# Pairwise bilinear products: the depth instead of the batch on the partitions, and input tiles loaded in four pieces behind stores

## The chip, the cores and the metric

The kernel runs on one core of a Trainium2 chip. The metric is the device time of one execution in microseconds (us): the median of three runs of the kernel before is 1301.92 us (1301.0 to 1302.68). A core has a matrix engine (PE, with its weight loads shown apart as PEld), a vector engine (DVE), a scalar engine (ACT), GpSimd (POOL) and a sync engine (SP) that here only issues transfers. Transfers between the device memory (HBM) and the on-chip memory (SBUF, 128 partitions) are carried by 16 DMA engines that all queues share. The matrix engine writes to a small accumulator memory (PSUM).

## What is computed

```python
def _L0_rec_ref(x, W):                    # x: (4096, 32, 64), W: (64, 64), float32
    vid = jnp.einsum('bfd,de->bfe', x, W)
    idx_i, idx_j = jnp.triu_indices(32, k=1)
    return x[:, idx_i, :] * vid[:, idx_j, :]
```

For each of 4096 batch rows, the 32 fields of depth 64 are projected by one 64 x 64 matrix, and each field i is multiplied, element by element, with the projection of each later field j. There are 496 such pairs. The input is 33.55 MB, the output 4096 x 496 x 64 floats, which is 520.09 MB. All is float32.

## The kernel before

**Tiles.** The batch lies on the partitions. A group g is 256 batch rows, two (r = 0, 1) on each partition, so that a partition holds 16 KB of input (R x F x D floats); there are 16 groups. The unit of work is a tile t = 2g + r: 128 batch rows, one on each partition, with 32 x 64 inputs and 496 x 64 outputs per partition. There are 32 tiles.

**Loads** (`load`, L62 to L73). The first three groups are loaded at the start on the sync queue, the first of them in three parts (L67, L68, L70). The other 13 are issued from ACT (L72), each after the second tile of the group three before, as one transfer of 2 MB with 16 KB per partition. Three buffers hold the groups.

**Projection** (`project`, L80 to L107). In a tile with the batch on the partitions the depth must first be brought onto the partitions. For each four pairs of fields, PE transposes four 128 x 128 blocks (L88), ACT copies them from PSUM to `xT` (L91), PE multiplies each field with W in float32 (two matmuls of 64 columns for a pair, on the upper and the lower 64 rows, L96), and ACT copies the result to `vid` (L103). `vid` has two buffers, so a tile's projection can run while DVE works on the tile before.

**Products** (`products`, L109 to L117). DVE does one multiplication for each field i: field i, repeated, times the projections of all later fields. That is 31 instructions to a tile.

**Stores.** The 496 pairs of a tile are cut by fields into three slots, `(0, 6)`, `(6, 13)` and `(13, 31)`: 171, 154 and 171 pairs. Each slot has its own output buffer from a pool of three, and is stored by one DMA on the sync queue (L137) once DVE has filled it. The first two tiles are stored in smaller parts (`FIRST`, `SECOND`).

**Order.** Within each engine the instructions run in program order. A store waits on SP for DVE's slot; DVE waits for the store that last used the slot's buffer. Loads from group 3 on wait in ACT's program among the copies, and travel in a queue of their own beside the stores' queue.

Of the kernel before, what the change touches and what calls it, by code (L numbers as in the profile page):

```python
# [1 line left out]

# [5 lines left out]

F32 = mybir.dt.float32
ALU = mybir.AluOpType  # L10

SLOTS = [(0, 6), (6, 13), (13, 31)]

FIRST = [(13, 31, [24, 18, 13]), (6, 13, [10, 8, 6]), (0, 6, [4, 2, 0])]
SECOND = [(0, 6, [2, 4, 6]), (6, 13, [8, 10, 13]), (13, 31, [18, 31])]


@with_exitstack  # L20
def pairwise_bilinear_kernel(
    ctx: ExitStack,
    tc: tile.TileContext,
    x: bass.AP,
    w: bass.AP,
    out: bass.AP,
):
    nc = tc.nc
    P = 128
    B, F, D = x.shape  # L30
    NP = F * (F - 1) // 2

    R = 2
    G = B // (P * R)


    TPB = 4
    GRP = F // 2 // TPB
    SLOT = 171
    AHEAD = 3  # L40

    xg = x.rearrange("(g p r) f d -> g p r f d", p=P, r=R)
    og = out.rearrange("(g p r) n d -> g p r n d", p=P, r=R)
    off = [i * (F - 1) - i * (i - 1) // 2 for i in range(F)]

    const = ctx.enter_context(tc.tile_pool(name="const", bufs=1))
    xpool = ctx.enter_context(tc.tile_pool(name="x", bufs=AHEAD))
    tpool = ctx.enter_context(tc.tile_pool(name="xT", bufs=1))
    vpool = ctx.enter_context(tc.tile_pool(name="vid", bufs=2))
    opool = ctx.enter_context(tc.tile_pool(name="out", bufs=3))  # L50
    ps_t = ctx.enter_context(
        tc.tile_pool(name="ps_t", bufs=4, space=bass.MemoryType.PSUM)
    )
    ps_v = ctx.enter_context(
        tc.tile_pool(name="ps_v", bufs=2, space=bass.MemoryType.PSUM)
    )

    w2 = const.tile([P, D], F32)
    nc.scalar.dma_start(out=w2[0:D, :], in_=w)
    nc.scalar.dma_start(out=w2[D : 2 * D, :], in_=w)  # L60

    def load(g):  # L62
        queue = nc.sync if g < AHEAD else nc.scalar
        xt = xpool.tile([P, R, F, D], F32, tag="x", name=f"x_{g}")
        if g == 0:
            h = F // 2
            nc.sync.dma_start(out=xt[:, 0, h:, :], in_=xg[g][:, 0, h:, :])  # L67
            nc.sync.dma_start(out=xt[:, 0, :h, :], in_=xg[g][:, 0, :h, :])  # L68
            for r in range(1, R):
                nc.sync.dma_start(out=xt[:, r], in_=xg[g][:, r])  # L70
        else:
            queue.dma_start(out=xt, in_=xg[g])  # L72
        return xt  # L73

    loaded = [load(g) for g in range(AHEAD)]

    ident = const.tile([P, P], F32)
    make_identity(nc, ident)

    def project(xt, r, tag, order):  # L80

        xT = tpool.tile([P, F // 2, P], F32, tag="xT", name=f"xT_{tag}")
        vid = vpool.tile([P, F // 2, 2, D], F32, tag="vid", name=f"vid_{tag}")
        for g in order:
            pairs = range(g * TPB, (g + 1) * TPB)
            pt = ps_t.tile([P, TPB, P], F32, tag="pt", name=f"pt_{tag}_{g}")
            for k, pair in enumerate(pairs):
                nc.tensor.transpose(  # L88
                    pt[:, k, :], xt[:, r, 2 * pair : 2 * pair + 2, :], ident
                )  # L90
            nc.scalar.copy(xT[:, g * TPB : (g + 1) * TPB, :], pt)  # L91

            pv = ps_v.tile([P, 2, 2 * TPB, D], F32, tag="pv", name=f"pv_{tag}_{g}")
            for k, pair in enumerate(pairs):
                for h in range(2):
                    nc.tensor.matmul(  # L96
                        pv[:, h, k, :],
                        lhsT=xT[h * D : (h + 1) * D, pair, :],
                        rhs=w2[h * D : (h + 1) * D, :],
                        start=True,  # L100
                        stop=True,
                    )
            nc.scalar.copy(  # L103
                vid[:, g * TPB : (g + 1) * TPB].rearrange("p k h e -> p h k e"),
                pv[:, :, :TPB, :],
            )
        return vid.rearrange("p g h e -> p (g h) e")  # L107

    def products(xt, vid, ot, base, r, fields):  # L109
        for i in fields:  # L110
            n = F - 1 - i
            nc.vector.tensor_tensor(  # L112
                ot[:, off[i] - base : off[i] - base + n, :],
                xt[:, r, i : i + 1, :].to_broadcast([P, n, D]),
                vid[:, i + 1 :, :],
                ALU.mult,
            )  # L117

    for g in range(G):
        xt = loaded[g]  # L120
        for r in range(R):
            t = g * R + r
            first = t == 0
            vid = project(xt, r, t, range(GRP - 1, -1, -1) if first else range(GRP))
            plan = FIRST if first else SECOND if t == 1 else None
            for s, (lo, hi) in enumerate(SLOTS):
                if plan:
                    lo, hi, ends = plan[s]
                else:
                    ends = [hi]  # L130
                ot = opool.tile([P, SLOT, D], F32, tag="o", name=f"o_{t}_{s}")
                base = off[lo]
                at = hi if first else lo
                for e in ends:
                    a, b = (e, at) if first else (at, e)
                    products(xt, vid, ot, base, r, range(b - 1, a - 1, -1) if first else range(a, b))
                    nc.sync.dma_start(  # L137
                        out=og[g][:, r, off[a] : off[b], :],
                        in_=ot[:, off[a] - base : off[b] - base, :],
                    )  # L140
                    at = e
        if g + AHEAD < G:
            loaded.append(load(g + AHEAD))


_INS = ["r_x", "L0_rec_W"]
_OUTS = [((4096, 496, 64), "float32")]


# [21 lines left out]
```

## Time and profile before

| what | value |
|---|---|
| median of three runs | 1301.92 us |
| the profiled execution's own time | 1302.08 us |
| its span, first to last instruction | 1300.3 us |
| DVE busy | 1132.8 us, 992 instructions |
| PE busy / PEld busy | 336.3 us / 315.8 us |
| ACT busy | 136.4 us |
| packets of the sync queue, of the ACT queue | 526.39 MB, 27.30 MB |

The page gives busy time by engine, then the span in 40 slices (busy tenths of each engine, the clock granted to PE, and what the DMA engines moved), then queues, the chain of work that ended last, the groups of instructions and the DMA issues. An engine's idle time is listed with what released it. A DMA's time runs from its issue to its landing, so it includes the time in which it stands in its queue.

### The profile page before, as it was taken

To read this page: it belongs to the slowest core of one execution; us is meant where nothing else is said; L and a number is where in the kernel's file an instruction comes from. 1 tells how busy PE (TensorE), PEld (TensorE's weight loads), DVE (VectorE), ACT (ScalarE), POOL (GpSimd) and SP (SyncE) were. 2 spreads that over 40 slices of the span, in tenths; PEclk is the share of its full clock that TensorE was granted. 3 is DMA by queue.
4 is the path that set the end of the run, shared out by engine and by line. 5 is a ranking of instruction groups with operands and counts; after the bars stand their busy time and mean duration, and the time that the engine had idled before them with its cause. 6 is when DMAs were issued, how large, how long until landed. Compare 5 with 4: busy or idle time off the path is not lost.

```text
span 1300.3 us, 6845 instructions
## 1 busy us (share of the span) xinstructions
PE 336.3 (26%) x2560; PEld 315.8 (24%) x2560; DVE 1132.8 (87%) x992; ACT 136.4 (10%) x257; POOL 0.7 (0%) x6
## 2 busy tenths in 40 slices
PE   7333213332033320333203332033330233321000
PEld 6333203332033320333203332033330223311000
DVE  6999979889798897988979899798987979999991
ACT  3111101111011110111101111001110011110000
POOL 0000000000000000000000000000000000000000
PEclk9555555555555555555555555555555555555555
DMA  9999999999999999999999999999999999999997
GB/s 384 430 421 439 428 430 436 423 432 430 428 429 430 434 422 436 435 422 433 433 429 431 423 434 424 430 435 428 433 426 427 437 421 430 434 433 431 436 431 318
DMA packets 18193, 554.12 MB, mean 426 GB/s; under 512 B 2160, under 2 KB 2160, under 8 KB 2544
## 3 DMA queue, kind: packets, MB, share of 16 engines
q1 hardware_dynamic: 16128, 526.39, 94.5%
q10 hardware_dynamic: 2032, 27.30, 4.9%
q8 instruction: 20, 0.33, 0.1%
q14 instruction: 13, 0.11, 0.0%
HBM read 33.59 MB, written 520.09 MB: 426 GB/s over the span
## 4 chain that ended last, share of the span: by engine, by line
DMA 62%; DVE 35%; issue 1%; PE 0%; DVEq 0%; ACT 0%
DMA out_dram<-o 61%; DVE o L112 35%; DMA x<-in_r_x_dram 0%; PE pt L88 0%; PE pv L96 0%; DVEq L166 0%; DVEq L112 0%; ACT vid L103 0%
## 5 line engine op out<-in xcount | busy, mean ns | idle before, releaser
L112 DVE TENSOR_TENSOR o<-x,vid 128x64 f32<-128x64 f32 (+30 forms) x992 | 1132.8, 1219 | 141.3 <-DMA out_dram<-o 130.2
L96 PE MATMUL pv<-w,xT 64*128 64x64 f32 x2048 | 230.0, 413 | 862.0 <-ACT vid L103 827.8
L96 PEld LDWEIGHTS pv<-w,xT 64*128 64x128 f32 x2048 | 218.2, 320 | 878.6 <-ACT vid L103 837.7
L103 ACT COPY vid<-pv 128x512 f32<-128x512 f32 x128 | 72.1, 587 | 1060.2 <-DVE o L112 971.3
L88 PE MATMUL pt<-ident,x 128*128 128x128 f32 x512 | 108.8, 397 | 5.4 <-DMA x<-in_r_x_dram 5.4
L88 PEld LDWEIGHTS pt<-ident,x 128*128 128x128 f32 x512 | 97.6, 212 | 9.0 <-issue 5.3
L91 ACT COPY xT<-pt 128x512 f32<-128x512 f32 x128 | 66.4, 610 | 5.7 <-PE pt L88 5.6
L91 ACT ACT_TABLE_LOAD x1 | 1.3, 1283 | 2.0 <-issue 2.0
masks.py:199 POOL TENSOR_SCALAR_AFFINE_SELECT ident<-ident 128x128 f32<-128x128 f32 x1 | 0.3, 292 | 0.1
masks.py:197 POOL MEMSET ident<- 128x128 f32 x1 | 0.2, 204 | 0.3 <-POOLq L157 0.3
L157 POOL MEMSET const-bfloat16-1.0<- 128x1 bf16 x1 | 0.1, 102 | 0.0
L157 POOL MEMSET const-uint8-127<- 128x1 uint8 x1 | 0.1, 102 | 0.0
L157 POOL MEMSET const-float32-0.0<- 128x1 f32 x1 | 0.1, 99 | 0.2 <-issue 0.2
L157 POOL MEMSET const-float32-1.0<- 128x1 f32 x1 | 0.1, 99 | 0.0
## 6 DMA issues: line engine op xcount, KB each, us to landing
out_dram<-o SPq DMA_DIRECT2D x60, 5472.0 KB, 25.5
out_dram<-o SPq DMA_DIRECT2D x30, 4928.0 KB, 28.4
x<-in_r_x_dram ACTq DMA_DIRECT2D x13, 2048.0 KB, 23.0
out_dram<-o SPq DMA_DIRECT2D x2, 2560.0 KB, 12.8
x<-in_r_x_dram SPq DMA_DIRECT2D x2, 2048.0 KB, 14.4
out_dram<-o SPq DMA_DIRECT2D x2, 1952.0 KB, 11.6
out_dram<-o SPq DMA_DIRECT2D x2, 1920.0 KB, 11.6
out_dram<-o SPq DMA_DIRECT2D x2, 1824.0 KB, 11.6
```

The costliest lines, as they stand in the source:

```text
L88: nc.tensor.transpose(pt[:, k, :], xt[:, r, 2 * pair : 2 * pair + 2, :], ident)
L91: nc.scalar.copy(xT[:, g * TPB : (g + 1) * TPB, :], pt)
L96: nc.tensor.matmul(pv[:, h, k, :], lhsT=xT[h * D : (h + 1) * D, pair, :], rhs=w2[h * D : (h + 1) * D, :], start=True, stop=True,)
L103: nc.scalar.copy(vid[:, g * TPB : (g + 1) * TPB].rearrange("p k h e -> p h k e"), pv[:, :, :TPB, :],)
L112: nc.vector.tensor_tensor(ot[:, off[i] - base : off[i] - base + n, :], xt[:, r, i : i + 1, :].to_broadcast([P, n, D]), vid[:, i + 1 :, :], ...
L157: nc = _bacc.Bacc("TRN2", target_bir_lowering=False, num_devices=1)
```

## The change

**Layout.** The depth now lies on the partitions. The input array is handed to the device as 16 tiles of 128 x 32 x 128: partition p below 64 holds depth p of one batch block of 128 rows, partition 64 + p depth p of another block 2048 rows on. The output is laid out likewise, 128 x 496 x 128 per tile, and brought back to the reference's order after the run. The rearrangement of both arrays is not part of the device's program. A tile is therefore twice as large: 32 x 128 inputs (16 KB) and 496 x 128 outputs per partition, and there are 16 tiles.

**Projection.** No transposes, no identity, no `xT`. W stands twice, on partitions 0 to 63 and 64 to 127. For each group of 8 fields PE does four matmuls of 512 columns (two field quads by two halves of the partitions), each 64 x 64 weights, and ACT copies the 1,024 results per partition to `vid` at once. Four groups make a tile.

**Products and stores.** The 496 pairs are cut into six slots of 83 pairs (the last of 81) whatever the field borders, with one store each, and still three output buffers. A slot holds 83 x 128 floats per partition, 42.5 KB. DVE has 36 instructions to a tile. The first tile is done backwards and stored in 14 smaller parts.

**Loads.** Everything goes through the sync queue, whose order is now that of the program text (`manual_schedule`). Tile 0 is loaded in four pieces of 8 fields, tile 1 in two. From tile 2 on, a tile comes in four pieces of 8 fields (4 KB per partition, 512 KB in all), piece n issued directly behind the store of slot n of the tile before, n = 1 to 4, slots being counted from 0. There are two input buffers instead of three.

The core of the diff:

```diff
-    R = 2
-    G = B // (P * R)
-    TPB = 4
-    GRP = F // 2 // TPB
-    SLOT = 171
-    AHEAD = 3
+    GRP = 8
+    NGRP = F // GRP
+    BANK = 512 // C
+    SLOT = 83
+    AHEAD = 2
+    PIECES = 4
...
+    ctx.enter_context(tc.manual_schedule(engines={mybir.EngineType.SP}))
...
+    def load(t, lo, hi):
+        if t not in xs:
+            xs[t] = xpool.tile([P, F, C], F32, tag="x", name=f"x_{t}")
+        nc.sync.dma_start(out=xs[t][:, lo:hi, :], in_=x[t][:, lo:hi, :])
...
-                nc.tensor.transpose(
-                    pt[:, k, :], xt[:, r, 2 * pair : 2 * pair + 2, :], ident
-                )
-            nc.scalar.copy(xT[:, g * TPB : (g + 1) * TPB, :], pt)
...
+            pv = psum.tile([P, GRP, C], F32, tag="pv", name=f"pv_{t}_{g}")
+            for b in range(0, GRP, BANK):
+                f = g * GRP + b
                 for h in range(2):
+                    half = slice(h * D, (h + 1) * D)
                     nc.tensor.matmul(
-                        pv[:, h, k, :],
-                        lhsT=xT[h * D : (h + 1) * D, pair, :],
-                        rhs=w2[h * D : (h + 1) * D, :],
+                        pv[half, b : b + BANK, :],
+                        lhsT=w2[half, :],
+                        rhs=xs[t][half, f : f + BANK, :],
                         start=True,
                         stop=True,
                     )
+            nc.scalar.copy(vid[:, g * GRP : (g + 1) * GRP, :], pv)
...
+        fields = [i for i in range(F - 1) if off[i] < b and off[i + 1] > a]
+        for i in reversed(fields) if backwards else fields:
+            s, e = max(a, off[i]), min(b, off[i + 1])
+            j = i + 1 + s - off[i]
             nc.vector.tensor_tensor(
+                ot[:, s - base : e - base, :],
+                xs[t][:, i : i + 1, :].to_broadcast([P, e - s, C]),
+                vid[:, j : j + e - s, :],
                 ALU.mult,
             )
...
+    for g in reversed(range(NGRP)):
+        load(0, g * GRP, (g + 1) * GRP)
+    load(1, F // 2, F)
+    load(1, 0, F // 2)
...
+            for n, base in enumerate(bases):
+                top = min(base + SLOT, NP)
+                ot = opool.tile([P, SLOT, C], F32, tag="o", name=f"o_{t}_{n}")
+                products(t, vid, ot, base, base, top)
+                store(t, ot, base, base, top)
+                if 1 <= n <= PIECES and t + 1 < NT and t + 1 not in (0, 1):
+                    load(t + 1, (n - 1) * F // PIECES, n * F // PIECES)
...
+    x = x.reshape(2, NT, C, F, D).transpose(1, 0, 4, 3, 2).reshape(NT, 2 * D, F, C)
```

## The prediction

> **What bounds the kernel now.** I read the page first: the busy shares, the DMA row of the 40 slices, the bytes, the chain.
>
> ```profile
> span 1300.3 us, 6845 instructions
> ...
> PE 336.3 (26%) x2560; PEld 315.8 (24%) x2560; DVE 1132.8 (87%) x992; ACT 136.4 (10%) x257; POOL 0.7 (0%) x6
> ...
> DMA  9999999999999999999999999999999999999997
> ...
> HBM read 33.59 MB, written 520.09 MB: 426 GB/s over the span
> ...
> DMA 62%; DVE 35%; issue 1%; PE 0%; DVEq 0%; ACT 0%
> ```
>
> The DMA engines are full in every slice but the last. DVE's 35% of the chain is no limit: the chain alternates between a store and the slot that it set free. The next view says so, the waits.
>
> ```profile
> DVE o L112 <- DMA out_dram<-o: 130.2, 71, 4.7
> ```
>
> DVE waits 130.2 us in all for stores to free buffers, so it has that much in hand. Bytes and bandwidth set the time, and the change moves the same bytes. Next, busy times by stretch, for stretches between the starts of a third slot; after the span the columns are PE, PEld, DVE, ACT and POOL busy (instructions), clock, DMA share, GB/s.
>
> ```profile
> 1111.63:1149.05 37.42, 10.74 (x80) 10.20 (x80) 35.38 (x31) 4.20 (x8) 0.00 (x0) 0.55 1.01 435
> 1149.05:1186.48 37.43, 7.36 (x64) 6.98 (x64) 35.38 (x32) 4.20 (x8) 0.00 (x0) 0.50 1.00 432
> 1030.32:1111.63 81.31, 21.23 (x160) 19.98 (x160) 70.94 (x62) 8.40 (x16) 0.00 (x0) 0.54 1.00 429
> ```
>
> The first two are single tiles after the last load: 16.25 MB of stores in 37.43 us, or 434.2 GB/s. The third is two tiles and one 2 MB load: 81.31 - 2 x 37.43 = 6.45 us for a load that at 434.2 GB/s would be 4.83. Over the chain from 182.33 to 1111.63 (23 tiles, 11.5 loads) a load costs (929.3 - 860.9) / 11.5 = 5.95 us.
>
> Then the DMA issues, for how deep the queue is (count, size, median us to landing):
>
> ```profile
> out_dram<-o SPq DMA_DIRECT2D x60, 5472.0 KB, 25.5
> x<-in_r_x_dram ACTq DMA_DIRECT2D x13, 2048.0 KB, 23.0
> ```
>
> A store of 12.9 us lands 25.5 us after its issue: when it is issued, one other store is still ahead. Loads run three groups ahead, and no DVE wait for a load or for `vid` is listed but one at the start. Last, the timeline of one projection (start, length), for prices:
>
> ```profile
> 1086.08 1.07 ACT L103 COPY vid<-pv 128x512 f32<-128x512 f32 x2 [35.68 <-DVE o L112]
> 1086.72 3.68 PE L96 MATMUL pv<-w,xT 64*128 64x64 f32 x32 [31.15 <-ACT vid L103]
> 1111.63 12.73 DVE L112 TENSOR_TENSOR o<-x,vid 128x1152 f32<-128x1152 f32 x18 [1.85 <-DMA out_dram<-o]
> 1124.92 22.65 DVE L112 TENSOR_TENSOR o<-x,vid 128x1984 f32<-128x1984 f32 x13 [0.56 <-DMA out_dram<-o]
> ```
>
> From the two DVE rows (10,944 elements in 18 instructions, 20,800 in 13) I solve 1.043 ns per element and 73 ns per instruction.
>
> **What the skill says.** The Trainium skill, "DMA: Bandwidth & Descriptors", section "Queues, rings and completion order": on each DMA engine a queue's descriptors are taken in ring order, and an engine goes round robin between queues. The trace agrees on the second: a load of 4.8 us of work takes 23.0 us to land beside the stores. The first is what I rest on for loads put into the stores' own ring; no run of before shows it. The same page, "Where 436 GB/s comes from": the fabric's ceiling is 435.2 GB/s. The 434.2 above agrees, so nothing is left to win on stores. "FP8 and Floating Point Precision", "TensorE Precision Notes": a true float32 matmul takes four passes; "TensorE: Matmul & The Clock Gate", Part 3: matmuls on different row groups overlap. 32 matmuls of 64 columns in 3.68 us at half clock are 115 ns each; four passes at the page's cold 1.2 GHz would be 213 ns alone, so pairs did overlap.
>
> **The change part by part.**
>
> *Removed: 512 transposes, 128 `xT` copies.* They stand beside DVE and DMA work (ACT idles 971 us for DVE), gain 0. In the open they would cost a tile its 16 transposes (3.4 us a burst) and four copies; they are not in the open.
>
> *DVE.* 16 x 496 x 128 elements at 1.043 ns are 1059.9 us; 581 instructions (41 in tile 0, 36 in each other) at 73 ns are 42.4: 1102 us instead of 1133. Per tile 68.9 us against 80 us of DMA: DVE isn't the bound, gain 0.
>
> *Stores.* Same bytes. A slot of 10,624 elements is 5.44 MB, 12.53 us at 434.2 GB/s; the last, 10,368, is 12.23. 0 net.
>
> *Loads, as work.* 14 tiles in 56 pieces of 512 KB, 1.21 us each. Before shows 5.95 us for 2 MB, mixed with stores; I take that, and an allowance of 0.2 for the shorter rows: 14 x 0.2 = +3. Lower end: in one ring the mixing excess of 1.1 goes, -15. Upper end: each piece, not each load, pays 1.1, so +3.3 a tile, +46.
>
> *SP.* Its 56 load issues cost some 0.35 us each, in a queue that waits for DVE most of the time; hidden by the stores queued ahead. But a piece is now behind its store's wait: it can't be issued before DVE finished slot n, and can't be served before store n is through.
>
> *The new wait, which decides.* Slot 0 of tile t+1 begins with field 0, whose 31 products need all of `vid`, so also fields 24 to 31: piece 4, which stands behind store 4 of tile t. When piece 4 lands, the ring holds store 5 alone, which was ready long before (DVE is held three buffers back). DVE stands still until the projection is done, then has a whole slot to compute before SP, queued behind it, can issue the next store. From the end of piece 4 in the ring:
> - receipt of the landing 0.4: the last store's last packet starts at 1297.0 to 1297.5 and takes 12.9 / 8 = 1.6, so ends at 1298.6 to 1299.1; it lands at 1274.2 + 25.3 = 1299.5.
> - PE wakes 0.1 later (first load landed at 0.74 + 4.5 = 5.2, PE started at 5.36).
> - Four matmuls of 512 columns: 2,048 columns, as many as the 3.68 us burst above. I take 3.7. Lower end 1.8, at full clock (or if the old burst was held by its weight loads); upper end 7.2, if the two halves don't overlap.
> - ACT's copy of 1,024: one of 512 takes 0.585 (0.535 back to back), so 0.585 + 512 x 0.833 ns at the ScalarE page's rate of one element per cycle ("ScalarE: Activation LUTs", section "What ACT_TABLE_LOAD costs") = 1.0; with hand-overs 1.2.
> - DVE slot 0: 10,624 x 1.043 ns + 3 x 73 ns = 11.3.
> - Issue to first packet 1.0 (first load issued at 0.74; first packet in the window 1.5 to 2.0).
>
> Sum 17.7 us. Store 5 covers 12.2. The DMA engines stand idle 5.5 us at each entry into tiles 2 to 15 (tile 1 is loaded at the start): 14 x 5.5 = +77. It does not come back later: after the gap the ring only refills, and at the end of the next tile the same piece stands there again. Within a tile there is no second gap: slot 1 takes 11.4 us and store 0 12.5.
>
> *Start and end.* DVE can begin at about 9.5 us instead of 11.15 (piece landed 5.2, W at 1.32 + 5.6 = 6.9, PE at full clock 1.8, copy 1.0), but the ring has 4.2 MB to load (9.7 us) instead of 6.3 before it needs stores, and small first stores follow each other about 1 us apart: I put +3. The end is as now (5.31 instead of 5.47 MB last).
>
> Sum on the profile's span: 1300.3 + 3 + 77 + 3 = 1383.3. The profiled execution took 1302.08, 1.8 more than its span, and 0.2 more than the median of the runs; so 1385.
>
> **Rivals.**
> - *Faster: pieces overtake.* If the reads of a piece proceed while the store ahead in the same ring is still being written, piece 4 lands up to 12.5 us earlier, with stores 4 and 5 to cover the chain: 24.8 against 17.7, no gap. The mixing excess may go too: 1302 + 3 + 3 - 15 = 1293. It decides from 5.5 us of overtaking on. For it: read and write are different directions. Against: ring order, and loads at the start landed one after another (4.5, 5.5, 7.5 us from issue).
> - *PE twice as slow.* The halves now write the same PSUM banks on different partitions; if they run one after the other, 7.2 instead of 3.7: +49, 1434.
> - *Pieces dear.* Each switch between store and load costs the 1.1: 1385 + 43 = 1428.
> - *It doesn't do what it says.* The instruction order of the changed program shows the pieces behind stores 1 to 4 and the waits as described, so no chance is put on this.
>
> **Numbers.** Forecast, the gap of 3.5 to 7 us a tile, 0.75 (its own range 1352 to 1410: PE at 1.8 gives -27, a cheaper load -15, not both likely in full; the upper side by symmetry of the load price); PE serial 0.13; dear pieces 0.07; overtaking 0.05. A measurement of this kernel tells about 0.2%, 2.6 us. Faster 0.04, within 0.2% 0.01, slower 0.95. Leaving out overtaking and the corners where two dear cases meet, the range is 1352 to 1434.
>
> **What would show it.** In the profile after: GB/s that dips once in about 86 us instead of a flat row; DVE idle for `vid` some 14 times, each ending with ACT's copy, which waited for PE, which waited for the load; 17 to 18 us from the end of piece 4 to the first packet of the next store; mean GB/s near 401. If DVE waits mainly for stores and the DMA row is full, the step with the wait is wrong. If the gap is there but other than 5.5, PE's burst is the first term to look at. If stretches with no gap move less than 429 GB/s, the price of pieces is.

## The result, and the profile after

The changed kernel takes 1416.14 us (median of four runs, 1414.2 to 1416.86), against 1301.97 us for the kernel before: a ratio of 1.0875, 95% interval 1.0856 to 1.0894. It is slower, by 114 us where 83 were forecast, and inside the stated range. The profiled execution took 1414.2 us, its span is 1412.3 us, 112.0 us longer than before's.

The page of the kernel after: span, busy times, the DMA row of the 40 slices with what was moved, the bytes, and the chain that ended last.

```profile
span 1412.3 us, 2185 instructions
...
PE 222.2 (16%) x512; PEld 56.7 (4%) x512; DVE 1099.4 (78%) x581; ACT 66.1 (5%) x65; POOL 0.2 (0%) x4
...
DMA  8999989799898998979979899798998979989799
GB/s 338 431 426 416 410 352 423 340 420 423 333 428 357 420 426 345 429 342 420 422 327 431 348 414 428 328 432 351 408 428 337 426 342 414 430 348 409 341 443 401
...
HBM read 33.59 MB, written 520.09 MB: 392 GB/s over the span
...
DVE 57%; DMA 27%; issue 9%; PE 4%; ACT 1%; SPq 0%; DVEq 0%
```

The bytes are the same. The row that was full is now full except for a dip to between 327 and 357 GB/s once in two or three slices, that is once a tile. In the chain the DMA share has fallen from 62% to 27%, and what is left of it is loads, not stores. The list of waits names the new one:

```profile
PE pv L72 <- DMA x<-in_r_x_dram: 1094.8, 56, 99.6
DVE o L88 <- ACT vid L79: 292.8, 15, 21.2
```

Before, DVE waited 130.2 us for stores and for `vid` only at the start. Now it never has to wait for a store; it waits for `vid` 15 times, the start and 14 entries into a tile, some 20 us each. The chain at one of them (start and length in us):

```profile
669.69 27.09 DMA x<-in_r_x_dram
...
696.91 3.69 PE pv L72 x8
...
700.63 1.02 ACT vid L79
...
701.67 0.04 DVE o L88
```

Piece 4 lands at 696.8, PE does its burst of matmuls, ACT its copy, and DVE starts slot 0 at 701.67. SP can issue the next store only when that slot is done, at 713.07. The stretches around it (columns as in the prediction: span, busy times of PE, PEld, DVE, ACT, POOL, then clock, DMA share, GB/s; a packet counts where it starts):

```profile
709.00:713.50 4.50, 0.00 (x0) 0.00 (x0) 4.50 (x3) 0.00 (x0) 0.00 (x0) 0.50 0.00 0
713.50:714.00 0.50, 0.00 (x0) 0.00 (x0) 0.50 (x2) 0.00 (x0) 0.00 (x0) 0.50 2.59 1105
```

For 4.5 us no DMA engine starts a packet, while DVE computes; then all start at once. The packet records of the whole run hold 14 stretches after the start in which no engine has a packet in flight, 5.0 to 5.2 us each.

From the landings in the trace I take the step from one transfer's last landing to the next one's. A tile's ten steps, mean over 13 tiles (s = store, l = load piece), and the same for three of the kernels below:

```
             s0     s1     l1    s2     l2    s3     l3    s4     l4    s5     tile
after        17.98  13.63  2.01  12.75  1.42  12.79  1.55  12.69  1.63  12.26  88.72
late         17.95  13.62  2.37+1.25+1.26  12.97  12.53  12.63  1.27  12.26    88.09
shift        13.44 (l 1.26)  13.46 (1.24)  13.49 (1.25)  13.47 (1.25)  12.55  12.24  83.66
bunch        12.55  12.55  1.23+1.56+1.25+1.35  12.68  12.54  12.54  12.24     80.50
```

In the last tile of the kernel after, which has no loads, stores 1 to 4 take 12.6 each. So store 0, with 17.98, carries a gap of 5.4 us. The rest of a tile is 83.3; six stores alone are 75.3; the 2 MB load costs 8.0 us in its four places, 6.6 in its own steps and 1.4 in the stores next to them. The account of the 112 us is then: gaps 14 x 5.4 = 75; loads 14 x (8.0 - 5.95) = 29; stores, 75.3 against 2 x 37.43 a tile, 16 x 0.44 = 7; together 111.

### The profile page after: what moved, and what is told of

It is laid out like the page before. It is cut to its first block, busy times and chain, and to the rows that moved or that the text cites. A ratio compares the mean times of both kernels' runs of the same rounds, so it can differ in the third digit from the quotient of the medians.

```text
span 1412.3 us, 2185 instructions
## 1 busy us (share of the span) xinstructions
PE 222.2 (16%) x512; PEld 56.7 (4%) x512; DVE 1099.4 (78%) x581; ACT 66.1 (5%) x65; POOL 0.2 (0%) x4
## 4 chain that ended last, share of the span: by engine, by line
DVE 57%; DMA 27%; issue 9%; PE 4%; ACT 1%; SPq 0%; DVEq 0%
DVE o L88 57%; DMA x<-in_r_x_dram 26%; PE pv L72 4%; ACT vid L79 1%; SPq L96 0%; DMA w<-in_L_rec_W_dram 0%; DVEq L154 0%
## 5 line engine op out<-in xcount | busy, mean ns | idle before, releaser
L88 DVE TENSOR_TENSOR o<-x,vid 128x1408 f32<-128x1408 f32 (+15 forms) x581 | 1099.4, 1973 | 292.8 <-ACT vid L79 292.8
L72 PE MATMUL pv<-x,w 64*64 64x512 f32 x512 | 222.2, 1013 | 1100.2 <-DMA x<-in_r_x_dram 1094.8
L79 ACT COPY vid<-pv 128x1024 f32<-128x1024 f32 x64 | 64.8, 1012 | 1255.4 <-PE pv L72 1255.4
L72 PEld LDWEIGHTS pv<-x,w 64*64 64x64 f32 x512 | 56.7, 206 | 1264.3 <-issue 1253.5
```

What stands on the lines that cost most here:

```text
L72: nc.tensor.matmul(pv[half, b : b + BANK, :], lhsT=w2[half, :], rhs=xs[t][half, f : f + BANK, :], start=True, stop=True,)
L79: nc.scalar.copy(vid[:, g * GRP : (g + 1) * GRP, :], pv)
L88: nc.vector.tensor_tensor(ot[:, s - base : e - base, :], xs[t][:, i : i + 1, :].to_broadcast([P, e - s, C]), vid[:, j : j + e - s, :], ALU ...
```

## Experiments

All keep the changed kernel's layout. Beside each median stands its ratio to the kernel before, taken in the same set of runs. In each of these kernels 14 tiles, 2 to 15, are loaded behind stores (13 where there is a third input buffer); in two expectations I took 15.

**shift: the pieces one store earlier.**

```diff
-                if 1 <= n <= PIECES and t + 1 < NT and t + 1 not in (0, 1):
-                    load(t + 1, (n - 1) * F // PIECES, n * F // PIECES)
+                if n < PIECES and t + 1 < NT:
+                    load(t + 1, n * F // PIECES, (n + 1) * F // PIECES)
```

> The same four pieces, one store earlier: behind stores 0 to 3, tile 2 starting it from tile 1. Gap theory (the DMA engines idle 5.4 us at each of 14 tile entries because only store 5 covers the chain piece 4 - projection - slot 0): stores 4 and 5 now cover 24.9 us against a chain of about 17.7, the gap goes, 1416 - 14 x 5.4 = 1340 us (1332 to 1350). Rival, the time is lost in the switches between stores and pieces and not in a gap: as many switches, so 1405 to 1416.

Measured 1343.63 us, ratio 1.0323 (1.0307 to 1.0338). As the gap theory said: 72.5 us of the 114 go with one place in the queue. DVE still waits for `vid` at every tile, but less than in the changed kernel, and waits for stores again:

```profile
DVE o L88 <- ACT vid L79: 135.5, 15, 11.6
DVE o L88 <- DMA out_dram<-o: 77.4, 27, 3.2
```

Of the first, nine us a tile are left. No stretch in which all engines are without a packet is left after the start, but a smaller gap is. From about 335 us on each tile has 1.1 to 2.4 us in which only two to four of the 16 engines have a packet in flight; one of them (at full use the DMA share, the last figure but one, is about 1):

```profile
753.30:754.90 1.60, 0.00 (x0) 0.00 (x0) 1.60 (x2) 0.00 (x0) 0.00 (x0) 0.50 0.12 52
```

A transfer gives 16 landing signals, which I take as one from each engine, and it has landed with the last of them. From about 335 us on the fifteenth signal comes 2 to 6 us after the fourteenth, and the last one 5 to 10 us after it. So piece 4 is late on two engines, DVE starts late, and the other 14 run out of work for a moment although stores 4 and 5 stand behind the piece. Averaged over the 16 engines this is 23 us of idle time between 180 and 1280 us, against 0.2 in the next kernel.

**bunch: all four pieces behind store 1.**

```diff
+                if n == 1 and t + 1 < NT:
+                    for m in range(PIECES):
+                        load(t + 1, m * F // PIECES, (m + 1) * F // PIECES)
```

> The four 512 KB pieces one after the other behind store 1, so one switch between stores and loads per tile instead of four, rows still of 4 KB. Gap theory: stores 2 to 5 cover the chain, no gap, at most 1340. If the excess of the pieces (8.0 us a tile, with what the stores before them lose, against 4.8 at the rate of the stores) is a price per switch: 1.5 us a tile once, about 1316. If it is a price of rows of 4 KB or of each DMA: as the four spread pieces, 1340.

Measured 1301.47 us, ratio 1.0000 (0.9991 to 1.0009). Lower than any of the expectations: as fast as the kernel before. The same four DMAs with the same 4 KB rows cost 42 us less than in shift. So neither the rows of 4 KB nor the number of DMAs is what makes the pieces dear in shift. Two things differ: there they stand apart, and the last of them stands two stores later. The run pairs, below, bears on both. DVE's list is that of a kernel bound by stores again:

```profile
DVE o L88 <- DMA out_dram<-o: 156.0, 85, 7.4
DVE o L88 <- ACT vid L79: 11.3, 1, 11.3
```

**one: the tile in one DMA with 16 KB per partition behind store 1.**

```diff
+                if n == 1 and t + 1 < NT:
+                    load(t + 1, 0, F)
```

> The whole tile of 2 MB in one DMA with 16 KB per partition behind store 1. If the price is per switch: as the bunch, about 1316. If it is per row or per DMA: the bunch at 1340 and this one near 1310 to 1316.

Measured 1311.25 us, ratio 1.0073 (1.0058 to 1.0088). Against expectation this form is dearer than the bunch, by 9.8 us over 14 tiles. That counts against my allowance for shorter rows in the prediction: it had the wrong sign. The edit changes two things, the length of the rows and the number of DMAs, and no run separates them. Much of the difference lies on few engines: by the signals of the last store 11 of 16 end by 1296.9 us and the last at 1308.3, in the bunch 13 by 1295.4 and the last at 1298.5.

**half: slot 0 stored in two halves.**

```diff
+                mid = base + 41 if n == 0 else top
+                products(t, vid, ot, base, base, mid)
+                store(t, ot, base, base, mid)
+                if n == 0:
+                    products(t, vid, ot, base, mid, top)
+                    store(t, ot, base, mid, top)
```

> Pieces stay behind stores 1 to 4; only slot 0 of each tile is stored in two halves (41 and 42 pairs), so that SP can issue after 5.7 us of DVE work instead of 11.3. Gap theory: the chain shrinks from 17.7 to 12.1, store 5 covers 12.2, the gap goes (0 to 0.5 us a tile), about 1340 to 1346. If the chain before the slot (landing, projection) is what counts, or something else holds the ring, nothing changes: 1412 to 1418.

Measured 1379.34 us, ratio 1.0597 (1.0581 to 1.0613): 37 us gained, half of what I expected, so neither reading holds as written. The landings say why. The first half comes without a gap (6.21 us, as much as it takes to carry), but store 1 now takes 16.4 us, and a gap stands there, in the trace at 708.3 for 2.6 us with no packet in flight on any engine:

```profile
709.00:710.50 1.50, 0.00 (x0) 0.00 (x0) 1.50 (x2) 0.00 (x0) 0.00 (x0) 0.50 0.00 0
711.00:724.00 13.00, 0.00 (x0) 0.00 (x0) 13.00 (x6) 0.00 (x0) 0.00 (x0) 0.50 0.93 377
```

DVE started at 688.68 and needs 22.7 us for slots 0 and 1, however they are stored; the issue takes 1.0 more, and 5.3 had passed since the end of piece 4: 29.0 us, for which store 5 and both halves give 12.2 + 12.6 us of cover. That leaves 4.2 us; measured are 3.9 (16.4 less a store of 12.55). What I had overlooked is the second slot: a late DVE must win back its lead slot by slot, at 12.5 - 11.4 us each. A finer first store moves the gap and shortens it, it doesn't remove it.

**twice: the last group's matmuls done twice.**

```diff
-                for h in range(2):
+                for h in [0, 1] * (2 if t > 1 and g == NGRP - 1 else 1):
```

> As the changed kernel, but from tile 2 on the matmuls of the last group of fields are done twice (the second time over the first), nothing else. Gap theory: that burst of 3.7 us stands in the open in each of 14 tile entries, so the gap grows from 5.4 to about 8.8 us: 1416 + 14 x 3.4 = 1464. If the projection is covered, 1416.

Measured 1444.26 us, ratio 1.1100 (1.1081 to 1.1119): 28 us more than the changed kernel, where 48 were expected. The direction shows that the burst stands in the open. The size follows from the burst: PE's busy time grew from 222.2 to 252.0 us, 29.8 us, and DVE's wait for `vid` from 292.8 to 324.2, 31.4 us.

```profile
1073.86 5.02 PE L72 MATMUL pv<-x,w 64*64 64x512 f32 x16 [11.00 <-DMA x<-in_r_x_dram]
...
1255.07 6.57 PE L72 MATMUL pv<-x,w 64*64 64x512 f32 x16 [10.89 <-DMA x<-in_r_x_dram]
```

A double burst takes 5.0 to 6.6 us, against 3.7 for a single one at half clock: 2.1 more on the mean over 14 tiles, and nearly each microsecond of it became one of time. My 3.4 took half clock throughout, but even in the longest of them the clock granted in the second half is 0.65.

**pairs: two pieces behind store 0, two behind store 2.**

```diff
+                if n in (0, 2) and t + 1 < NT:
+                    for m in range(n, n + 2):
+                        load(t + 1, m * F // PIECES, (m + 1) * F // PIECES)
```

> The four pieces in two pairs, behind stores 0 and 2 of the tile before. With four separated pieces and no gap (shift) 1343.6 us, with one bunch 1301.5. If the price is per switch between stores and loads, the 42 us lie on three switches in each of 15 tiles, 0.94 each, and two switches give 1315.5 (1310 to 1320). If the 42 us come from the late landing of the last piece (DVE starts each tile late, the faster engines run dry), this one, with three stores behind its last piece, gives 1301 to 1305.

Measured 1308.67 us, ratio 1.0055 (1.0040 to 1.0070): 7.2 us above the bunch, 0.5 us for one more separate place a tile, between the two expectations. A fixed price of 0.94 per place (1.0 with 14 tiles) falls. Three more places, as in shift, would be 21 of its 42 us at this price. The rest goes with the two engines that lag: in shift 14 of the 16 engines end their last store by 1332.9 us, two at 1336.2 and 1340.1, while in pairs all end within 3 us, and between 180 and 1280 us at least 12 engines have a packet in flight. So the second reading holds in part, too: in shift the faster engines do run dry. But the late ones don't, and why two engines lag there, and fewer or less elsewhere, is not shown.

**late: pieces 1 to 3 behind store 1, piece 4 behind store 4.**

```diff
+                if n in (1, 4) and t + 1 < NT and t + 1 not in (0, 1):
+                    for m in range(3) if n == 1 else [3]:
+                        load(t + 1, m * F // PIECES, (m + 1) * F // PIECES)
```

> The changed kernel's gap with half its separate places: pieces 1 to 3 together behind store 1, piece 4 alone behind store 4 as in the changed kernel. If gap and piece price add up: the gap of 5.4 us stays (14 x 5.4 = 76), the pieces cost their 4.8 at the stores' rate and about 1.6 more in two places instead of 3.2 in four, so 1416 - 14 x 1.6 = 1394 (1385 to 1400). If the pieces' price belongs to the gap (all DMA engines in step after it), it stays 1410 to 1416; if there is no gap but only a price of separate places, about 1309, as the two pairs.

Measured 1402.87 us, ratio 1.0784 (1.0769 to 1.0799), 12 us less than the changed kernel by the ratios, where 22 were expected. The gap is the same (17.95 in the table). Two places fewer save 0.9 us a tile (0.6 in the profiled executions of the table) and not 1.6. The table shows what stays: store 1 at 13.62 and a first piece at more than 2 us, in both kernels. These belong to the first load after the gap; later places cost about 0.5 or less, as do the first ones in pairs, where there is no gap. So the price of the pieces partly belongs to the gap.

**actq: the bunch from ACT's queue; actone: one DMA of 16 KB rows from there.**

```diff
+                if n == 1 and t + 1 < NT:
+                    for m in range(PIECES):
+                        load(t + 1, m * F // PIECES, (m + 1) * F // PIECES, nc.scalar)
```

> The bunch of four pieces, issued from ACT and so in a ring of its own [...]as the loads of the kernel before. If mixing with stores row by row is what makes a load dear (5.95 us for 2 MB in the kernel before, 5.4 for the bunch in the stores' ring), 1301.5 + 15 x 0.6 = about 1310. If each change between a store's row and a load's row had the price of 0.94, it would be far dearer, above 1340. If only the ring's order matters for nothing, 1301.5.

> The whole tile in one DMA of 16 KB per partition from ACT's ring, against the same bytes in four DMAs of 4 KB per partition from the same ring (1298.3). If rows of 16 KB make a load dearer (in the stores' ring one DMA took 1311.3, four took 1301.5), about 1307, and the kernel before, whose loads have that form, pays for the same reason. If the number of bytes alone counts in a ring of its own, 1298.

actq measured 1298.26 us, ratio 0.9977 (0.9968 to 0.9987); actone 1305.61 us, ratio 1.0033 (1.0019 to 1.0046). Loads issued from ACT into a ring of their own are not dearer, as I had thought, but cheaper by 3 us, though the moment of issue differs too (see the last section). One DMA of 16 KB rows costs 7 us more there too. The kernel before loads in just that form; how much of its own 5.95 us for a load comes from it was not tried.

**ahead: a third input buffer, the bunch two tiles ahead; aheadq: the same from ACT's queue.**

```diff
-    AHEAD = 2
+    AHEAD = 3
...
+    for m in range(PIECES):
+        load(2, m * F // PIECES, (m + 1) * F // PIECES)
...
+                if n == 1 and t + 2 < NT:
+                    for m in range(PIECES):
+                        load(t + 2, m * F // PIECES, (m + 1) * F // PIECES)
```

> The bunch, with a third input buffer: three tiles are loaded at the start, and each later tile comes in one bunch behind store 1 two tiles before. The steady tiles cost the same 80.5 us; the start, where the ring stands idle for some 2.9 us between small stores while DVE has just begun, has 2 MB more to carry in that time. Expected 1297 to 1300, if the start's idle time is filled; 1301.5 if it isn't.

> The two cheaper forms together: a third input buffer with loads two tiles ahead (1296.4 us) and the four pieces from ACT's own ring (1298.3 against 1301.5 in the stores' ring). If their gains of 5.1 and 3.2 us add: 1293. If they save the same time: 1296.

ahead measured 1296.39 us, ratio 0.9960 (0.9945 to 0.9975), aheadq 1292.89 us, ratio 0.9935 (0.9923 to 0.9948). The two gains add. Between 15 and 30 us the bunch has three stretches with no packet in flight, 2.9 us together; ahead has none, as expected. aheadq is the fastest version here, 8.7 us below the kernel before, with the row full from the first slice:

```profile
span 1291.1 us, 2172 instructions
...
DMA  9999999999999999999999999999999999999998
...
HBM read 33.59 MB, written 520.09 MB: 429 GB/s over the span
```

So the layout with the depth on the partitions isn't what lost the time; the places of the loads in the queue are.

## Why the prediction was right, and where its sizes were off

*Removed transposes and copies, DVE.* Forecast at no gain. DVE is busy 1099.4 us (1102 forecast) and PE a third less, and neither shows in the time of any kernel above in which the DMA row is full.

*The new wait.* Right, in mechanism and in size, the size in part by luck. Shift and twice show the mechanism from two sides: take the chain's cover up by one store and the gap of all engines is gone (one in which 14 engines idle for 1 to 2 us stays); lengthen the chain by 2.1 us and store 0 takes 20.0 us instead of 17.98. The terms: PE 3.69 us (3.7 taken); ACT 1.01 (1.0); start of DVE 4.9 us after the landing; issue of store 0 at 713.07, 16.3 after the landing, and the first packet after 713.5. The gap is 5.4 us against 5.5, 75 us against 77. The sentence that within a tile there is no second gap holds for this kernel; half shows that it holds only because store 0 comes so late.

That PE's term came out is luck. I equated the new burst with the old one as having the same 2,048 columns. But the 32 of the old burst are records, and the program has 1,024 such matmuls (32 in each of 32 tiles) for the 2,048 records of the page:

```profile
L96 PE MATMUL pv<-w,xT 64*128 64x64 f32 x2048 | 230.0, 413 | 862.0 <-ACT vid L103 827.8
```

So the old burst had 16 matmuls and 1,024 columns, 230 ns a matmul and not 115, and the reading that pairs overlap, which I had from the 115, does not follow. The new burst took the same time for twice the columns. At the old price per column it would have been 7.4 us, about the rival's figure, and the gap 9 us. The old burst was held by something other than its columns, perhaps by its weight loads (busy 3.49 of its 3.68 us, against 0.84 in the new one); no run tests that. In the new burst the eight records, of four matmuls, start two by two, 7 to 40 ns apart, and each lasts about 1.06 us: two run at a time, and the rival with a serial PE falls.

*Loads, as work.* This is the term that was mis-sized: "14 x 0.2 = +3" was 29, which is 26 of the 31 us by which the forecast fell short. I took the load's price from the kernel before, 5.95 us for 2 MB, and added only for row length. It is 8.0 in four separate places. The upper bound that I had named, 1.1 more per piece, would have been 9.3; the truth lies between the forecast and the rival with dear pieces. Longer rows in one DMA were dearer, not cheaper (one, actone). What counts is how many places the loads stand in between stores (bunch, pairs, shift), whether the first of them follows a gap (late), and how far single engines lag (shift).

*Stores.* Forecast at 0. They took 12.6 us each in step after a gap and 12.53 to 12.55 in bunch and shift: 7 us in all that no step had.

*Start.* Forecast +3. Tile 0 has landed at 94.0 us; less its stores (2 x 37.43 = 74.9) and 4.2 MB of loads (9.7) that leaves 9.4 us. In the kernel before the same remainder is 1299.4 - 32 x 37.43 - 13 x 5.95 - 14.5 for the first 6.3 MB = 9.8 us. So the start cost nothing.

*Overtaking.* The rival on the faster side falls: piece 4 landed 1.6 us after store 4 (l4 in the table), not before it. This agrees with the Trainium skill, "DMA: Bandwidth & Descriptors", section "Queues, rings and completion order", by which each DMA engine takes a queue's descriptors in ring order.

**What stays open.** Why loads that stand apart are dear, and why some engines lag. The packet records give hints. In the changed kernel 213 of the 11,520 store rows of tiles 1 to 15 took over 0.3 us longer than the median for their size, and during 87% of them a load row began, against 16% of all store rows. In the bunch there are 23 such rows, in actq 7. But a ring of their own does not by itself spare the stores: there are 149 in actone and 147 in the kernel before, whose loads also come from ACT, in rows of 16 KB, and about nine in ten of them meet a load row. Engines that lag matter in every kernel without the gap: in the kernel before the 16 engines end between 1289.1 and 1299.4 us, and the last one is the kernel's time, so differences of a few us between these kernels can lie on one engine. Neither the long store rows, nor the lag, nor the dearer DMA of 16 KB rows, nor why the first load after a gap costs 2 us more, has a cause that a run here shows.

## What to carry to other kernels

In these kernels a load that shares a queue with stores is as late as the store ahead of it, so count what stands behind it: the transfers queued after its last piece must last longer than everything from its landing to the first packet of the next store. Here that is 17.6 us (a cover of 12.2 and a gap of 5.4). The consumer must win back its lead for later slots too, and a transfer lands only when the slowest DMA engine is through. A place one store earlier was worth 72 us, and the pieces kept together behind store 1 another 42. Splitting a load to spread it out is not free even where every byte is covered; price it from a stretch of the profile in which loads and stores meet.

## What the runs showed that I had not expected

- Four loads of 512 KB together behind one store cost 5.4 us for 2 MB; the same four apart cost 8.0 with a gap in the tile, and a tile in shift, where no gap of all engines is left, is 3.2 us longer than in bunch.
- The 16 DMA engines drift apart. In shift two of them were up to 10 us behind, and the other 14 ran dry for 1 to 2 us in each tile while those two were still at work.
- One DMA with rows of 16 KB was dearer than four with rows of 4 KB for the same tile: 1311.25 against 1301.47 us in the stores' ring, 1305.61 against 1298.26 in a ring of their own.
- The same loads from ACT's ring instead of the stores' ring saved 3.2 us (1298.26 against 1301.47) and 3.5 us (1292.89 against 1296.39). The skill's page on DMA, section "Issuing engines are not separate DMA queues", says that spreading the issue over engines saves only the sequencer's time; here SP was not short of time, and in the first pair the intervals of the ratios don't overlap (in the second they just do). From ACT the loads are also issued at another moment, when the input buffer comes free and not behind store 1; which of the two brings the gain was not tried.
